# A planner's pace, and stages that are held behind their loads, in a four-layer network whose recurrent scans run beside everything else

## The chip, the cores and the metric

The kernel runs on one core of a Trainium2 chip. The metric is the device time of one launch in microseconds (us), as the median of several runs. A profile is one further execution, recorded by the hardware profiler.

The core's engines each take their instructions strictly in the order of their own queue: TensorE (PE, matmuls; its weight loads are shown as PEld), VectorE (DVE), ScalarE (ACT), GpSimd (POOL) and SyncE (SP). Nearly every DMA of this kernel is issued by SP, so SP's queue orders the transfers, and a wait in it holds back every load behind it.

## The reference, cut to what matters

Four layers work on four images of 1024 positions and 256 channels each. Layers 0 and 3 hold a recurrent scan; layer 1 is a grouped convolution, layer 2 is masked attention and a mixture of eight experts, layer 3 ends with another mixture.

```python
# layer 0, after a norm, a projection to 512 channels, a 3x3 convolution and gelu (x below; N = 64)
dt = softplus(dt_raw @ w_dt + dt_bias);  A = -exp(A_log)
def step(h, inp):                     # 1024 steps for each image
    xt, dtt, Bt, Ct = inp
    h = exp(dtt[:, :, None] * A) * h + (dtt * xt)[:, :, None] * Bt[:, None, :]
    return h, einsum('bdn,bn->bd', h, Ct)
y = ys + x * D_skip                   # then norm, @ w_out, + src
# layer 1: 1x1, grouped 3x3 and 1x1 convolutions with relu, + x
# layer 2: 8 heads; scores where mask else -inf; softmax; @ V; @ Wo; norm; then 8 experts, top 2
# layer 3: x_main, x_gate = split(t @ W_in);  the same kind of scan (N = 16) on silu(x_main @ W_conv)
y = y_seq * silu(x_gate)              # then @ W_out, + t, then 8 experts, top 2
```

## The kernel before, in words

**The scans.** `scans` (L339) runs eight scans one after the other, in the order of `SCANS` (L31): layer 0's for images 0 to 3 and layer 3's for images 0 to 3, here called (0,0), (0,1), (3,0), (0,2), (3,1), (0,3), (3,2), (3,3). A scan is cut into units of 128 rows (channel and state) by 1024 positions: 256 units for layer 0, 64 for layer 3, 1280 in all. For one unit

- SP loads the decay exponents, `dA` (two loads of 256 KB for layer 0, eight of 64 KB for layer 3; five buffers, issued four units ahead),
- ACT takes their exponential two units ahead,
- PE spreads the input over the states into `ps_rep`, one unit ahead (two PSUM buffers),
- DVE multiplies `ps_rep` by B and then scans: the two half steps of a unit, with a `yield` after each,
- POOL multiplies the result `h` by C, and PE collects two units at a time into `ps_y`; ACT copies that out to `yo`.

**The stages.** Everything else is written as generators that yield after a small piece of work, a tick. `STAGES` (L33) lists them: `front` 1 to 3 (layer 0 up to the scan), `middle` 0 to 3 (layer 0's end in `back0`, then `layer1`, `attention`, `moe`, and layer 3 up to its scan in `front3`), `last` 0 to 2 (layer 3's end in `back3`, then `moe`). A stage starts when the scan named beside it is done. The scan and the stages are recorded in one order by hand (a manual schedule): what stands earlier on an engine runs earlier.

**The planner.** `run` (L503) goes through the scan's half steps. It keeps a clock for each of PE, DVE, ACT and POOL: `Metered` (L88) adds an estimated cost for every instruction that is recorded, `matmul_us` (L67) for matmuls. After each half step a clock that is more than `LAG` behind DVE's is pulled up to that distance, and then at most `TICKS` ticks are taken, as long as no clock is ahead of DVE's:

```python
now = clock["vector"]
for e in clock:
    clock[e] = max(clock[e], now - LAG)
for _ in range(TICKS):
    if max(clock.values()) > clock["vector"] + LEAD or self.advance() is None:
        break
```

The value that a tick yields is not used to pace it. When the next scan's inputs are not ready, `need` (L478) takes ticks without pause until they are; the order then has a stretch in which no scan work stands. What is left after the last scan is taken in one go, and `last` for image 3 follows alone, outside the manual schedule.

**The places that the change touches.** `front` (L636) loads x and two weights, sets two pads to zero and goes on to a norm. `back0` (L743) has SP issue 14 loads: the image `tb` (1 MB), the scan's sums `y_back` (eight loads, 2 MB), `u_back` (four, 2 MB) and `w_out` (0.5 MB); two empty ticks follow, then POOL adds rows to `tb`, and DVE adds u times a factor to `y_back`, four instructions. `back3` (L1615) does the same with `gate_back` in the place of u, and POOL multiplies `y_back` by it. `scanned` (L736) issues the `y_back` loads. `attention` (L1048) projects q, k and v, lets POOL add rows to two tiles, and calls `shift` (L1119). That takes the squared norms of q and k on ACT and PE, reduces them on DVE to one number, `large`, which PE, DVE, ACT and SP read into registers (L1159) and branch on (L1161); the other arm is not taken with this data. Only then does SP issue the load of `maskT` (L1101, 2 MB), and `heads` (L1231) runs: for each pair of heads and each of eight key blocks one tick of scores (PE matmuls `ps_sc`, the mask added by a matmul, ACT's exponential `p`) and one of values (`ps_at`). After every two pairs DVE takes a reciprocal of `sums`. `steps` (L540) prepares a scan's inputs: ACT for the softplus (`sp_r`, `sp_e`, `sp_l`), DVE and POOL for its parts, ACT and DVE again for a split into three bf16 parts (`sp_x`, `parts`).

In the profile nearly all of these instructions stand at L120, the line of `Metered` that records them, so groups are told apart by their tiles.

Of the kernel before, what the change touches and what calls it, by code (L numbers as in the profile page):

```python
# [8 lines left out]
BF16 = mybir.dt.bfloat16  # L9
# [7 lines left out]
P = 128  # L17
NB = 4
L = 1024
TB = L // P  # L20
C = 256
DI = 512
DC = DI // P
# [16 lines left out]

LEAD, LAG, TICKS = 0.0, 4.0, 2

# [13 lines left out]
def columns(x):  # L60
    n = 1
    for k in x.shape[1:]:
        n *= k
    return n


def matmul_us(out, lhsT=None, rhs=None, **_):  # L67
    if lhsT is None:
        lhsT = out
    us = 0.46e-3 * columns(out)  # L70
    if lhsT.dtype != BF16:
        us = max(4 * us, 0.3)
    if out.shape[0] <= 32:
        return us / 4
    return us / 2 if lhsT.shape[0] <= 32 else us


def by_columns(per, fixed, of=0):
# [9 lines left out]
class Metered:  # L88
# [21 lines left out]
    def __getattr__(self, key):  # L110
        got = getattr(self.what, key)
        if self.name is None:
            return Metered(got, self.clock, key) if key in self.COST else got
        cost = self.COST[self.name].get(key)
        if cost is None:
            return got

        def run(*args, **kw):
            self.clock[self.name] += cost(*args, **kw)
            return got(*args, **kw)  # L120

        return run


class Hybrid:
# [352 lines left out]
    def need(self, scan):  # L478

        late = False  # L480
        while ("parts", *scan, DC - 1) not in self.ready:
            if self.advance() is None:
                raise RuntimeError(f"{scan} waits for a stage that waits for it")
            late = True
        if late:

            self.clock.update(dict.fromkeys(self.clock, max(self.clock.values())))

    def advance(self):

        if self.stage is None:
            can = [x for x in self.todo if x[2] is None or x[2] in self.done]
            if not can:
                return None
            self.todo.remove(can[0])
            self.stage = getattr(self, can[0][0])(can[0][1])
        cost = next(self.stage, None)
        if cost is None:
            self.stage = None
            return 0.0  # L500
        return cost

    def run(self):  # L503

        self.done, self.ready = set(), set()
        self.todo, self.stage = list(STAGES), None
        nc, tc = self.nc, self.tc
        with tc.tile_pool(name="fps", bufs=1, space=PSUM) as pp:
            self.side_psum(pp)
            for _ in self.front(0):  # L510
                pass
            self.mask_prepare()
        with tc.tile_pool(name="scan", bufs=1) as mp, tc.tile_pool(
            name="scps", bufs=1, space=PSUM
        ) as psum, tc.tile_pool(name="sdps", bufs=1, space=PSUM) as side, tc.manual_schedule():
            self.side_psum(side)
            scatter = self.scatter()
            clock = self.clock = dict.fromkeys(Metered.COST, 0.0)
            self.nc = Metered(nc, clock)
            for n, _ in enumerate(self.scans(mp, psum)):  # L520
                if n % 2:
                    next(scatter, None)
                now = clock["vector"]
                for e in clock:
                    clock[e] = max(clock[e], now - LAG)
                for _ in range(TICKS):
                    if max(clock.values()) > clock["vector"] + LEAD or self.advance() is None:
                        break
            while self.advance() is not None:
                pass  # L530
            self.nc = nc
        assert not self.todo
        with tc.tile_pool(name="lps", bufs=2, space=PSUM) as pp:
            self.side_psum(pp)
            for _ in self.last(NB - 1):
                pass
# [99 lines left out]
    def front(self, b):  # L636
        nc, tc, vec = self.nc, self.tc, self.vec
        R, N = 16, 64
        key = (0, b)
        with tc.tile_pool(name=f"f{b}", bufs=1, side="right") as op:  # L640
# [4 lines left out]
            with tc.tile_pool(name=f"fa{b}", bufs=1, side="right") as fp:  # L645
# [3 lines left out]
                pads = [fp.tile([P, 34, 34], F32, name=f"pad{i}") for i in range(2)]  # L649
                for i in range(2):  # L650
                    nc.gpsimd.memset(pads[i], 0.0)
                yield 1.0
                xT = fp.tile([P, 2, L], F32, name="xT0")
                yield from self.norm(fp, x, TB, x, "ln1")
                yield from self.turned(x, TB, xT, (vec["L0_conv_ln1_g"], vec["L0_conv_ln1_b"]))
# [77 lines left out]
    def image(self, flat, b):  # L733
        return flat[b * L : (b + 1) * L, :].rearrange("(j p) c -> p j c", p=P)

    def scanned(self, pool, key):  # L736
        y = pool.tile([P, DC, L], F32, name="y_back")
        for d in range(DC):
            for c in range(2):
                self.nc.sync.dma_start(y[64 * c : 64 * c + 64, d, :], self.mem["y", *key, d, c])  # L740
        return y

    def back0(self, b, tb):  # L743


        nc, tc, vec = self.nc, self.tc, self.vec
        with tc.tile_pool(name=f"k{b}", bufs=1, side="right") as sp:
            nc.sync.dma_start(tb, self.image(self.a["x"].rearrange("b h w c -> (b h w) c"), b))
            y = self.scanned(sp, (0, b))
            u = sp.tile([P, DC, L], F32, name="u_back")  # L750
            for d in range(DC):
                nc.sync.dma_start(u[:, d, :], self.mem["u", 0, b, d])
            w_out = sp.tile([P, DC, C], F32, name="w_out0")
            nc.sync.dma_start(w_out, self.mem[("w_out0",)])
            yield 2.0
            yield 2.0
            yield from self.add_rows(tb, self.bout0, TB)
            for d in range(DC):
                nc.vector.scalar_tensor_tensor(
                    y[:, d, :], u[:, d, :], vec["L0_conv_D_skip"][:, d : d + 1], y[:, d, :],  # L760
                    ALU.mult, ALU.add,
                )
                yield 1.3
            mv = sp.tile([P, TB, 2], F32, name="b0mv")
            got = {}

            def turn(j):
                got[j] = ps = self.ps("ps_yt")
                for d in range(DC):
                    nc.tensor.transpose(  # L770
                        ps[:, d * P : (d + 1) * P], y[:, d, j * P : (j + 1) * P], self.ident
                    )

            def stats(j):
                st = sp.tile([P, 6], F32, tag="b0st", name="b0st", bufs=2)
                nc.vector.bn_stats(st, got.pop(j))
                nc.vector.bn_aggr(mv[:, j, :], st)

            yield from self.pipe(range(TB), turn, stats, cost=1.0)
            r = self.rstd(sp, mv[:, :, 1], 1e-5, TB, "b0")  # L780
            yield 0.8

            def project(j):
                got[j] = ps = self.ps("ps_o")
                for d in range(DC):
                    nc.tensor.matmul(
                        ps[:, :C], lhsT=y[:, d, j * P : (j + 1) * P], rhs=w_out[:, d, :],
                        start=(d == 0), stop=(d == DC - 1),
                    )

            def add(j):
                nc.vector.scalar_tensor_tensor(
                    tb[:, j, :], got.pop(j)[:, :C], r[:, j : j + 1], tb[:, j, :], ALU.mult, ALU.add
                )

            yield from self.pipe(range(TB), project, add, cost=1.7)
# [251 lines left out]
    def attention(self, b, tb):  # L1048
        nc, tc, vec = self.nc, self.tc, self.vec
        with tc.tile_pool(name=f"at{b}", bufs=1, side="right") as op:  # L1050
# [3 lines left out]
            v = op.tile([P, TB, C], F32, name="v")  # L1054
            mT = op.tile([P, 2, L], BF16, name="mT")
            wo = self.weight(op, "L2_attn_Wo", 2)
            with tc.tile_pool(name=f"aa{b}", bufs=1, side="right") as fp:
                wq, wk, wv = (self.weight(fp, "L2_attn_" + n, 2) for n in ("Wq", "Wk", "Wv"))
                xT = fp.tile([P, 2, L], F32, name="xTa")
# [32 lines left out]
                    nc.scalar.copy(v[:, 2 * j : 2 * j + 2, :], ps)  # L1092

                yield from self.pipe(range(TB // 2), values, cost=1.7)
            yield from self.add_rows(xa, self.bo, TB)
            yield from self.add_rows(tb, self.beta, TB)
            with tc.tile_pool(name=f"ab{b}", bufs=1, side="right") as fp:
                yield from self.shift(fp, qT, kT, mT)
            with tc.tile_pool(name=f"ac{b}", bufs=1, side="right") as fp:
                maskT = fp.tile([P, TB, L], BF16, name="maskT")  # L1100
                nc.sync.dma_start(maskT, self.mem[("maskT",)].rearrange("j p f -> p j f"))  # L1101
                yield 1.0
                for nh in range(2):
                    raw, sums = (
                        fp.tile([P, 2, 512], F32, tag=t, name=t) for t in ("raw", "sums")
# [13 lines left out]
    def shift(self, fp, qT, kT, mT):  # L1119
# [30 lines left out]
        nc.vector.tensor_scalar(most[:, 0:1], most[:, 0:1], -1.0, 1.0, ALU.mult, ALU.add)  # L1150
        large = fp.tile([1, 1], I32, name="large")
        nc.vector.tensor_copy(large, most[:, 0:1])
        yield 1.0
        yield 1.0
        E = mybir.EngineType
        go = {
            E.PE: nc.tensor, E.DVE: nc.vector, E.Activation: nc.scalar, E.SP: nc.sync,
# [457 lines left out]
    def back3(self, b, tb):  # L1615
        nc, tc = self.nc, self.tc
        with tc.tile_pool(name=f"h{b}", bufs=1, side="right") as sp:
            nc.sync.dma_start(tb, self.mem["t", b])
            y = self.scanned(sp, (3, b))
            gate = sp.tile([P, DC, L], F32, name="gate_back")  # L1620
            for d in range(DC):
                nc.sync.dma_start(gate[:, d, :], self.mem["gate", b, d])
            w_out = self.weight(sp, "L3_attn_W_out", DC)
            yield 2.0
            yield 2.0
            for d in range(DC):
                for g in range(2):
                    cols = slice(g * 512, (g + 1) * 512)
# [101 lines left out]
```

## Time and profile before

| what | us |
|---|---|
| median of 3 runs (7048.52 to 7061.61) | 7055.18 |
| profiled execution, whole | 7061.6 |
| its span, first to last instruction | 7059.5 |
| busy: PE, DVE, ACT, POOL | 5383.6, 5212.0, 3462.1, 3650.0 |
| DVE: 1280 scans of 2.285 | 2924.7 |
| DVE: 1280 multiplies of 1.213 | 1553.0 |
| first scan starts; last POOL product of a scan ends | 317.7; 6646.1 |

The span has five parts: a start without scans (to 318 us), a long stretch in which units follow each other (to 5743), a stall in which scan (3,3) waits for its inputs (to about 6250), the rest of the scans (to about 6643), and a tail in which PE ends the experts of images 2 and 3. A line of a timeline has the start and length in us, the engine, the source line, the operation, its output and inputs with their shapes, and in brackets the idle time of the engine before it with what ended that. A line of a table of waits has the engine and tile that waited, what it waited for, and then the us in total, the times and the longest. "issue" is idle time that ended with nothing the profile can name.

### The profile page before, as it was taken

Reading aid. Unit: us, or ns where it says so; the run is one execution under the profiler, and the core shown is the slowest. Engines: PE = TensorE matmul, PEld = TensorE weight load, DVE = VectorE, ACT = ScalarE, POOL = GpSimd, SP = SyncE. Lnnn points to the kernel's source line nnn. Section 1 sums busy time; section 2 is a strip of 40 time slices with the busy share of each in tenths; the row PEclk is TensorE's granted clock in tenths of the full one; section 3 lists DMA queues with packets and bytes.
Section 4 is the critical chain, followed back from the end, with each engine's and each line's share of the span. In section 5 each row is a group of like instructions: output and inputs, shape, how many; then the busy total and the mean of one; then the engine's idle time right before and its main releaser. Section 6 shows DMA issues by size and latency. Waiting matters only on the chain. (4 is left out here: it accounts for less than half of the span.)

```text
span 7059.5 us, 66331 instructions
## 1 busy us (share of the span) xinstructions
PE 5383.6 (76%) x20516; PEld 2218.2 (31%) x20516; DVE 5212.0 (74%) x4477; ACT 3462.1 (49%) x4162; POOL 3650.0 (52%) x1801
## 2 busy tenths in 40 slices
PE   7185876578898567879779668898698677957979
PEld 3020221032253022224235332242254322513556
DVE  2787898887898986789889877898899831247511
ACT  3254666244477324447658434577386332244511
POOL 1288677664556754555766554556656520045300
PEclk9585876578888567979879778898698889877989
DMA  2355666654456565446656654456666620135421
GB/s 82 77 139 158 161 178 167 169 143 120 115 143 176 160 172 136 119 116 171 176 151 164 178 144 120 115 143 178 165 168 165 162 70 6 44 107 152 113 63 33
DMA packets 395053, 939.03 MB, mean 133 GB/s; under 512 B 83268, under 2 KB 165776, under 8 KB 393040
## 3 DMA queue, kind: packets, MB, share of 16 engines
q1 hardware_dynamic: 392512, 932.10, 49.0%
q8 instruction: 172, 2.82, 0.2%
q0 software_dynamic: 2128, 2.13, 0.2%
q14 instruction: 241, 1.97, 0.1%
HBM read 844.17 MB, written 93.95 MB: 133 GB/s over the span
## 5 line engine op out<-in xcount | busy, mean ns | idle before, releaser
L120 POOL TENSOR_TENSOR h<-h,rows 128x1024 f32<-128x1024 f32 x1280 | 3024.2, 2365 | 2138.8 <-DVE h L120 1756.0
L120 DVE TENSOR_TENSOR_SCAN h<-dA,ps_rep 128x1024 f32<-128x1024 f32 x1280 | 2924.7, 2285 | 228.0 <-issue 94.6
L120 DVE TENSOR_TENSOR ps_rep<-ps_rep,rows 128x1024 f32<-128x1024 f32 x1280 | 1553.0, 1213 | 338.7 <-PE ps_rep L120 317.0
L120 ACT ACTIVATE dA<-dA,A_L_conv_A_log 128x1024 f32<-128x1024 f32 x1024 | 1152.8, 1145 | 695.2 <-DMA dA<-dt 600.6
L120 PE MATMUL ps_rep<-S,spread_L_conv_A_log 96*128 96x512 bf16 x2048 | 763.2, 463 | 899.6 <-DVE h L120 731.7
L120 PE MATMUL ps_y<-h,collect_L_conv_A_log 128*32 128x512 f32 x4096 | 750.2, 755 | 91.1 <-POOL h L120 91.1
L120 ACT ACT_TABLE_LOAD x494 | 633.8, 1283 | 174.7 <-DMA dA<-dt 115.0
L120 PEld LDWEIGHTS <-spread_L_conv_A_log 96*128 96x128 bf16 x2048 | 164.5, 103 | 1661.3 <-DVE h L120 1213.5
L120 PE MATMUL ps_h<-xTm,we 128*128 128x512 f32 x1280 | 605.2, 609 | 7.6 <-ACT h_m L120 6.6
L120 PE MATMUL ps_e<-we,h_m 128*128 128x256 f32 x2560 | 587.9, 381 | 10.1 <-ACT h_m L120 10.1
L120 ACT ACTIVATE p<-ps_sc 128x512 f32<-128x512 f32 x512 | 277.9, 595 | 587.2 <-PE ps_sc L120 573.8
L120 ACT ACTIVATE dA<-dA,A_L_attn_A_log 128x1024 f32<-128x1024 f32 x256 | 293.6, 1148 | 490.1 <-DMA dA<-dt 456.4
L120 PEld LDWEIGHTS ps_e<-we,h_m 128*128 128x128 f32 x2560 | 481.8, 190 | 140.6 <-issue 46.0
L120 PE MATMUL ps_at<-p,v 128*32 128x512 f32 x1024 | 363.6, 627 | 63.1 <-ACT p L120 55.7
L120 PE MATMUL ps_rep<-S,spread_L_attn_A_log 96*128 96x512 bf16 x512 | 191.4, 464 | 280.8 <-DVE h L120 239.2
L120 ACT ACTIVATE h_m<-ps_h,cols 128x512 f32<-128x512 f32 x320 | 216.5, 687 | 302.2 <-PE ps_h L120 299.3
L120 DVE SCALAR_TENSOR_TENSOR tb<-ps_e,cw,tb 128x256 f32<-128x256 f32 x448 | 192.6, 473 | 200.5 <-PE ps_e L120 200.5
L120 PEld LDWEIGHTS ps_h<-xTm,we 128*128 128x128 f32 x1280 | 242.4, 193 | 288.1 <-issue 236.3
L120 PE MATMUL ps_sc<-qT,kT 32*128 32x512 f32 x1024 | 300.7, 663 | 0.0
L120 PE MATMUL ps_at<-p,ones 128*32 128x512 f32 x1024 | 280.1, 627 | 0.0
L120 DVE RECIPROCAL sums<-sums 128x512 f32<-128x512 f32 x16 | 53.6, 3353 | 253.4 <-ACT sums L120 253.4
L120 PEld LDWEIGHTS ps_y<-h,collect_L_conv_A_log 128*32 128x32 f32 x4096 | 98.8, 119 | 450.4 <-issue 234.3
(406 smaller groups left out, 5703.5 us busy)
## 6 DMA issues: line engine op xcount, KB each, us to landing
dA<-dt SPq DMA_DIRECT2D x2048, 256.0 KB
dA<-dt SPq DMA_DIRECT2D x2048, 64.0 KB
we<-in_L_ffn_W_dram SPq DMA_DIRECT2D x64, 512.0 KB
parts<-parts SPq DMA_DIRECT2D x64, 384.0 KB
S<-parts SPq DMA_DIRECT2D x96, 256.0 KB
dt<-sp_r SPq DMA_DIRECT2D x64, 256.0 KB
y<-yo SPq DMA_DIRECT2D x128, 128.0 KB
y_back<-y SPq DMA_DIRECT2D x64, 256.0 KB
```

The costliest lines, as they stand in the source:

```text
L120: return got(*args, **kw)
```

## The change

Five edits:

1. The planner's costs and pace. A matmul's cost gets a fixed part; those with few rows get other factors. `LAG` goes from 4 to 8, and `HEAVY` is new: after a tick that moved any clock by more than 1.5 us, no second tick follows in the same half step.
2. `Hold`: a tick can yield `Hold(n)`, and for n half steps no tick is taken, unless the planner is forced to (in `need`, and after the last scan).
3. `Hold` stands in the place of empty ticks: 8 half steps after the loads of `front`, 4 after those of `back0` and 4 more after its row additions, 5 before the branch in `shift`, 8 after the loads of `back3`.
4. In `back0` and `back3` the loads of `y_back` and of u or gate go out in turns: two of `y_back` and one of the other for each quarter. Their number and size stay.
5. `maskT` moves into a pool that lives through the whole of `attention`, and its load is issued after the projections, before the row additions and `shift`.

```diff
-LEAD, LAG, TICKS = 0.0, 4.0, 2
+LEAD, LAG, TICKS, HEAVY = 0.0, 8.0, 2, 1.5
...
-    us = 0.46e-3 * columns(out)
+    us = 0.07 + 0.42e-3 * columns(out)
     if lhsT.dtype != BF16:
-        us = max(4 * us, 0.3)
+        us = max(4 * us - 0.23, 0.3)
     if out.shape[0] <= 32:
-        return us / 4
-    return us / 2 if lhsT.shape[0] <= 32 else us
+        return 0.28 * us
+    return 0.6 * us if lhsT.shape[0] <= 32 else us
...
+class Hold(int):
+    pass
...
-    def advance(self):
+    def advance(self, forced=False):
+        if self.half < self.until and not forced:
+            return None
...
+        if isinstance(cost, Hold):
+            self.until = self.half + cost
         return cost
...
+                self.half = n
                 for _ in range(TICKS):
+                    before = dict(clock)
                     if max(clock.values()) > clock["vector"] + LEAD or self.advance() is None:
                         break
-            while self.advance() is not None:
+                    if max(clock[e] - before[e] for e in clock) > HEAVY:
+                        break
+            while self.advance(forced=True) is not None:
...
-                yield 1.0
+                yield Hold(8)
                 xT = fp.tile([P, 2, L], F32, name="xT0")
...
-    def scanned(self, pool, key):
+    def scanned(self, pool, key, other, of):
         y = pool.tile([P, DC, L], F32, name="y_back")
         for d in range(DC):
             for c in range(2):
                 self.nc.sync.dma_start(y[64 * c : 64 * c + 64, d, :], self.mem["y", *key, d, c])
+            self.nc.sync.dma_start(other[:, d, :], of(d))
         return y
...
-            y = self.scanned(sp, (0, b))
             u = sp.tile([P, DC, L], F32, name="u_back")
-            for d in range(DC):
-                nc.sync.dma_start(u[:, d, :], self.mem["u", 0, b, d])
+            y = self.scanned(sp, (0, b), u, lambda d: self.mem["u", 0, b, d])
...
-            yield 2.0
-            yield 2.0
+            yield Hold(4)
             yield from self.add_rows(tb, self.bout0, TB)
+            yield Hold(4)
...
             wo = self.weight(op, "L2_attn_Wo", 2)
+            maskT = op.tile([P, TB, L], BF16, name="maskT")
...
                 yield from self.pipe(range(TB // 2), values, cost=1.7)
+            nc.sync.dma_start(maskT, self.mem[("maskT",)].rearrange("j p f -> p j f"))
             yield from self.add_rows(xa, self.bo, TB)
...
             with tc.tile_pool(name=f"ac{b}", bufs=1, side="right") as fp:
-                maskT = fp.tile([P, TB, L], BF16, name="maskT")
-                nc.sync.dma_start(maskT, self.mem[("maskT",)].rearrange("j p f -> p j f"))
-                yield 1.0
...
         nc.vector.tensor_copy(large, most[:, 0:1])
-        yield 1.0
-        yield 1.0
+        yield Hold(5)
...
-            y = self.scanned(sp, (3, b))
             gate = sp.tile([P, DC, L], F32, name="gate_back")
-            for d in range(DC):
-                nc.sync.dma_start(gate[:, d, :], self.mem["gate", b, d])
+            y = self.scanned(sp, (3, b), gate, lambda d: self.mem["gate", b, d])
             w_out = self.weight(sp, "L3_attn_W_out", DC)
-            yield 2.0
-            yield 2.0
+            yield Hold(8)
```

More of the change, by code (lines that the diff above doesn't have):

```diff
@@ L481, in need @@
         while ("parts", *scan, DC - 1) not in self.ready:
-            if self.advance() is None:
+            if self.advance(forced=True) is None:
                 raise RuntimeError(f"{scan} waits for a stage that waits for it")
@@ L505, in run @@
         self.done, self.ready = set(), set()
+        self.half = self.until = 0
         self.todo, self.stage = list(STAGES), None
```

## The prediction

> **What bounds the kernel now.** I read four views: the busy table over stretches cut where the scan's first multiply stops and starts, VectorE's (DVE's) waits in the scan stretch, single timelines around the places that the change touches, and the waits of one place where no consumer blocks. The table's columns are stretch, length, then busy time of PE, weight loads, DVE, ACT and POOL, granted clock, DMA share, GB/s.
>
> ```profile
> 317.70:5743.00 5425.30, 4191.12 (x16349) 1610.91 (x16350) 4626.53 (x3571) 2927.38 (x3412) 3326.22 (x1606) 0.80 0.57 152
> 5743.00:6250.00 507.00, 428.75 (x1597) 183.26 (x1596) 75.26 (x179) 159.50 (x267) 39.52 (x31) 0.92 0.08 26
> 6250.00:6643.00 393.00, 261.80 (x965) 116.90 (x963) 294.32 (x238) 204.04 (x216) 213.99 (x107) 0.76 0.57 151
> 6643.00:7059.50 416.50, 372.04 (x1321) 251.63 (x1320) 59.01 (x150) 76.22 (x114) 17.05 (x13) 0.93 0.15 48
> ```
>
> In the first row DVE works 4626.5 of 5425.3 us: a unit of the scan is a 1.21 us multiply and a 2.28 us scan, so 3.5 us at best. The 799 us of DVE idle there are all that the change can win in this stretch. The second row is the stall before scan (3,3), where PE runs stage middle 3 alone; the last is the tail. The planner lays both versions out when the program is built; from that layout I take only which half step a tick falls in, never a time. It forces 306 ticks in the stall before and 307 after, and leaves 48 and 47 for after the last scan: these two rows stay. DVE's instructions stay the same too, so only the idle counts:
>
> ```profile
> DVE ps_rep L120 <- PE ps_rep L120: 283.8, 191, 15.7
> DVE sp_x L120 <- ACT parts L120: 58.7, 23, 14.2
> DVE y_back L120 <- DMA u_back<-u: 55.0, 4, 14.5
> DVE sums L120 <- ACT sums L120: 41.2, 12, 7.9
> ...
> DVE y_at L120 <- PE ps_wo L120: 17.8, 10, 2.2
> DVE ps_rep L120 <- DMA dA<-dt: 16.1, 3, 5.9
> ...
> DVE tb L120 <- PE ps_o L120: 14.5, 6, 5.4
> ...
> DVE ps_rep L120 <- issue: 5.4, 2, 5.2
> DVE ln_st L120 <- DMA x<-in_x_dram: 4.9, 2, 3.2
> ```
>
> The 283.8 us are PE's queue being late with the scan's input: a mask that has not landed, norms in `shift`, attention.
>
> **Holds at back0 and back3: little or nothing.** Each of the four back0 starts shows 12.6 to 14.5 us of DVE waiting for u (55.0 together). A hold takes this wait away. But SP issues 14 loads there (1 + 2 + 2 + 0.5 MB) ahead of the next dA rows, and the scan needs those. Middle 1, ACT and then DVE:
>
> ```profile
> 2537.35 1.15 ACT L120 ACTIVATE dA<-dA,A_L_attn_A_log 128x1024 f32<-128x1024 f32 x1 [1.50 <-DMA dA<-dt]
> 2563.25 1.15 ACT L120 ACTIVATE dA<-dA,A_L_attn_A_log 128x1024 f32<-128x1024 f32 x1 [24.76 <-DMA dA<-dt]
> ```
>
> ```profile
> 2553.29 2.52 DVE L120 SCALAR_TENSOR_TENSOR y_back<-u_back,cols,y_back 128x1024 f32<-128x1024 f32 x2 [13.81 <-DMA u_back<-u]
> ...
> 2564.34 2.27 DVE L120 TENSOR_TENSOR_SCAN h<-dA,ps_rep 128x1024 f32<-128x1024 f32 x1
> ```
>
> The next dA is ready at 2564.4, and DVE scans it at once. Without the u wait DVE would scan what it has (2539.5 + 2.29 + 1.21 = 2543.0) and wait 21 us for dA; today it waits 13.8 and uses the rest for four u sums (7.1 us). So the hold loses about 7 us here; taking the sums and u in turns moves no byte forward for dA. Stage last 2 shows it pure, since nothing on DVE needs its loads:
>
> ```profile
> DVE h L120 <- DMA dA<-dt: 24.2, 3, 21.8
> ```
>
> Middle 0 runs beside a scan with two loads a unit and ACT two units ahead: DVE would wait from 1405.6 to 1421.3, 15.7 for 12.6, +3. Sum +3 + 3 x 7 = **+24 us**; bounds -55 (the wait just goes) and +32 (four times 8). Back3 in last 0 and last 1: POOL waits for gate, PE for POOL, DVE 11.3 to 12.1 us for PE, then dA: it landed 2.3 us before ACT took it, so **-4** (0 to -26). [...]
>
> **Mask loaded as attention begins: -34 us.** PE waits for it with the scan's input queued behind:
>
> ```profile
> 2768.39 1.01 PE L120 MATMUL ps_sc<-maskT,identb 128*128 128x512 bf16 x2 [10.44 <-DMA maskT<-maskT]
> ```
>
> DVE loses 11.8, 15.6, 15.5 and 15.7 us (58.6). Now the 2 MB go out 14 half steps (25 us) earlier; the row needs 9.2 us from issue (2759.2). But dA queues behind: beside the scans of layer 3 (middles 1 to 3, eight dA loads a unit, SP without a gap) ACT finishes dA 0.2 to 0.4 us before DVE takes it, so some 8 us stay each; beside (0,1) about 1. 58.6 - 25 = 34; bounds 20 and 58.6.
>
> **Hold(5) before the branch: -4 us.** DVE loses 4.9 to 5.9 us at each of four branches. In the first, `large` is written at 1589.57 and read at once; the next DVE work starts at 1597.1. That is the branch, which stays; what goes is SP's wait of 6.8 us for `large`, with dA queued behind it. Bounds 0 and -20.
>
> ```profile
> L1726 PEldq COMPARE_BRANCH  x12: 163/314/5113, 594.3 to 5687.0; - x12
> ```
>
> On PE one such branch lasts 5.1 us. [...]
>
> **Pace of attention (new matmul costs): -38 us.** In `heads`, without the mask, DVE loses 39 + 45 + 47 us in middles 0 to 2. Steadily one key block runs per unit, and PE starts one every 4.0 us (2783.0, 2787.1, 2791.0, 2795.1), 0.97 of it the scan's own; DVE needs 3.7. The layout now spreads 16 blocks over 17.5 units instead of 15: 3.03 x 16/17.5 + 0.97 = 3.74, so the 0.3 us a unit nearly go: 14 to 2 us a middle; `sums` saves 3, since its values tick stands a half step earlier; bursts after pauses grow by 3. 12 x 3, and 2 for the part of middle 3: 38. The extra units are idle ones now, and cost DVE nothing. Bounds 0 and -110.
>
> **One heavy tick a half step: -18 us.** `ps_o`, `y_at` and `ps_e` (14.5, 17.8 and 15.9 us) are DVE waits for a matmul group issued in the same half step. One more half step (1.8 us) between them saves up to 1.8 in each of some 15 large ones, 27; I take 18. Bounds 0 and -48.
>
> **LAG 8: +37 us.** An idle engine may now owe 8 us instead of 4, though time that PE or ACT sat idle does not come back. In `steps` the ticks stand at half steps 0 2 4 6 8 10 15 instead of 0 2 4 6 11 17: ten more close ticks in six passes. A close one costs DVE 2.5 to 2.7 us (`sp_x` in middle 1): +25. Other starts (16 row additions in 4 half steps instead of 10, projections 13 instead of 16): +12. Bounds 0 and +45 for the first; the second is the slower rival's.
>
> **Small ones.** Hold at front: -5 (`ln_st`; the floor is 0). Tail: the eight POOL products (9.8 us) can start with the first gate: -4 (0 to -7).
>
> Sum: -34 - 4 - 4 - 38 - 18 - 5 - 4 = -107, +24 + 37 = +61, **-46 us**. The profiled execution took 7061.6, 6.4 above the median 7055.2 of the runs: 7061.6 - 46 = **7015 us**.
>
> **Rivals.** *The holds do free the scan.* For it: 78 us of DVE wait at back0 and back3 go. Against: last 2's 24.2. If dA comes in time, back0 and back3 are worth -55 and -23 instead of +24 and -4: 98 lower, **6917**. Or `heads` wins all of its bound (-110 for -38): **6943**.
> *Nothing to measure:* attention's waits are only moved, since PE is busy 943 of 1127 us in the scans that it stands beside. Without the -38: **7053**.
> *Slower, by the credit.* LAG 8 lets PE or ACT work bunch after each pause; the input of the scan has two buffers, so DVE stalls beyond 3.5 us of lateness. Some 36 starts after a pause (8 in each of 3.3 middles, and the fronts and lasts), each with up to 4 us more: 144, of which 37 are counted: 7015 + 107 = **7122**. It decides from 2.6 us a start (94 in all, 57 more than counted: 7072). For it: 14.2 us lost to ACT at one tick of front 1. Against: one heavy tick a half step, the two-tick cap.
>
> **How the numbers follow.** A measurement tells about 0.2% (14 us) from no change. Forecast (6970 to 7041) 0.45; holds or attention win more (below) 0.22; nothing (7041 to 7069) 0.15; slower 0.18. Faster 0.67, same 0.15, slower 0.18. The range 6930 to 7085 leaves some 0.1 out on each side; the forecast's own range is 6970 to 7041.
>
> **What would show it.** Right: no wait for u_back, but dA waits of 15 to 22 us on DVE at each back0; no PE wait for maskT; 5 us still lost at each branch; `ps_rep` from PE down by 90 to 130 us; `sp_x` from ACT up by some 20; the stall near 507 and the tail near 416 us. Wrong: if DVE's dA waits stay near 24 us in the scan stretch (the holds win), if `ps_rep` grows (the credit decides), or if the stall moves.

## The result, and the profile after

The changed kernel takes 7097.2 us (median of four runs), the kernel before beside it 7058.4: ratio 1.006, 95% interval 1.0034 to 1.0087. It is **0.6% slower**, where 7015 us was forecast. The profiled execution took 7118.0 us with a span of 7116.2, 21 above the median, so sums over its rows come out some 20 us above the runs.

First the busy table over the four stretches, cut as before (PE, weight loads, DVE, ACT, POOL, granted clock, DMA share, GB/s).

```profile
315.60:5805.00 5489.40, 4191.09 (x16280) 1595.69 (x16356) 4644.77 (x3571) 2838.52 (x3344) 3332.22 (x1606) 0.80 0.58 150
5805.00:6312.00 507.00, 426.50 (x1582) 183.39 (x1594) 75.29 (x179) 161.60 (x270) 41.45 (x33) 0.92 0.08 27
6312.00:6699.00 387.00, 255.26 (x957) 116.33 (x956) 295.32 (x238) 191.32 (x205) 212.79 (x105) 0.75 0.60 153
6699.00:7116.20 417.20, 374.30 (x1324) 253.14 (x1322) 58.56 (x150) 76.61 (x115) 17.07 (x13) 0.93 0.16 48
```

Stall and tail stay (507.0 for 507.0 us, 417.2 for 416.5). The scan stretch is 64 us longer. DVE runs the same 3571 instructions there, but is busy 18.2 us longer, and idle 46 us longer (844.6 for 798.8). DVE's waits there (total us, times, longest):

```profile
DVE ps_rep L120 <- PE ps_rep L120: 244.2, 139, 7.9
...
DVE sp_x L120 <- ACT parts L120: 84.1, 31, 6.8
DVE h L120 <- DMA dA<-dt: 79.0, 120, 17.7
DVE top L120 <- PE ps_n L120: 67.9, 4, 18.2
DVE h L120 <- ACT dA L120: 54.7, 54, 16.7
DVE y_at L120 <- PE ps_wo L120: 24.1, 12, 5.6
...
DVE tb L120 <- PE ps_e L120: 22.3, 25, 3.9
...
DVE ps_rep L120 <- DMA dA<-dt: 14.5, 3, 4.9
...
DVE sums L120 <- ACT sums L120: 12.0, 12, 2.1
```

Gone are the u waits (55.0) and most of sums (41.2 to 12.0); ps_rep lost 40. In their place came dA by DMA (24.4 to 79.0), dA by ACT (16.1 to 54.7), top (14.5 to 67.9: DVE waits for PE, which waits for ACT's squares in shift) and sp_x (58.7 to 84.1). Three of the four branches still cost 14.5 us (the row of ps_rep behind dA by DMA; each of them stands where the branch does). At back0 of middle 1, ACT and then DVE:

```profile
2569.59 1.15 ACT L120 ACTIVATE dA<-dA,A_L_attn_A_log 128x1024 f32<-128x1024 f32 x1 [1.53 <-DMA y<-yo]
2597.48 1.15 ACT L120 ACTIVATE dA<-dA,A_L_attn_A_log 128x1024 f32<-128x1024 f32 x1 [26.74 <-DMA dA<-dt]
```

```profile
2581.30 1.21 DVE L120 TENSOR_TENSOR ps_rep<-ps_rep,rows 128x1024 f32<-128x1024 f32 x1
2598.72 2.29 DVE L120 TENSOR_TENSOR_SCAN h<-dA,ps_rep 128x1024 f32<-128x1024 f32 x1 [16.21 <-DMA dA<-dt]
```

DVE multiplies, then stands 16.2 us for dA, which lies behind the bulk loads (SP issues those from 2568.7 to 2582.3, the next dA loads from 2584.2): the new wait that the forecast named.

### The profile page after: what moved, and what is told of

It is laid out like the page before. It is cut to its first block, busy times and chain, and to the rows that moved or that the text cites. A ratio compares the mean times of both kernels' runs of the same rounds, so it can differ in the third digit from the quotient of the medians.

```text
span 7116.2 us, 66199 instructions
## 1 busy us (share of the span) xinstructions
PE 5374.9 (76%) x20426; PEld 2203.0 (31%) x20516; DVE 5230.8 (74%) x4477; ACT 3363.1 (47%) x4086; POOL 3656.7 (51%) x1801
## 5 line engine op out<-in xcount | busy, mean ns | idle before, releaser
L120 DVE TENSOR_TENSOR ps_rep<-ps_rep,rows 128x1024 f32<-128x1024 f32 x1280 | 1553.7, 1214 | 283.8 <-PE ps_rep L120 263.1
L120 PE MATMUL ps_h<-xTm,we 128*128 128x512 f32 x1280 | 620.9, 616 | 19.2 <-ACT h_m L120 19.2
```

## The experiments

Beside each time stands the ratio to runs of the kernel before on the same chip. Three numbers are worked out from each run's trace: **stall**, from the end of the last scan instruction ahead of the gap to the first behind it (534.1 us before, 532.4 changed); **tail**, from the last scan to the end (416.0 and 417.1); **scans**, the rest from the first scan to the last (5791.7 and 5851.1). **Forced** counts the ticks that `need` takes in the stall; like every half step named below it comes from the layout, as in the forecast. Numbers "in the profiles" compare single executions; the changed kernel's is 21 us above its median, so differences against it below that size are weak.

| run | us | ratio (95%) | scans | stall | tail | forced |
|---|---|---|---|---|---|---|
| changed | 7097.2 | 1.0060 (1.0034-1.0087) | 5851.1 | 532.4 | 417.1 | 307 |
| e1_lag4 | 7126.5 | 1.0099 (1.0082-1.0115) | 5713.3 | 670.5 | 429.7 | 404 |
| e4_old_planner | 7148.9 | 1.0142 (1.0126-1.0157) | 5840.3 | 560.6 | 424.7 | 317 |
| e5_planner_alone | 7060.6 | 1.0012 (1.0003-1.0021) | 5821.7 | 523.0 | 404.7 | 300 |
| e6_mask_alone | 7036.9 | 0.9978 (0.9969-0.9987) | 5772.7 | 535.4 | 416.3 | 306 |
| e7_paced | 7100.6 | 1.0063 (1.0050-1.0076) | 5827.9 | 541.2 | 420.2 | 309 |
| e8_no_back_holds | 7053.5 | 0.9999 (0.9989-1.0008) | 5805.8 | 520.8 | 404.5 | 300 |
| e9_hold5 | 7084.9 | 1.0044 (1.0031-1.0057) | 5787.5 | 558.5 | 423.7 | 319 |
| e3_old_costs | 7207.6 | 1.0223 (1.0209-1.0236) | 5969.5 | 530.1 | 405.4 | 300 |
| e10_thin_pool | 7026.6 | 0.9961 (0.9948-0.9974) | 5747.3 | 535.3 | 417.8 | 307 |
| e2_no_cap | 7120.3 | 1.0096 (1.0082-1.0111) | 5863.1 | 529.5 | 411.3 | 305 |
| e12_turns_mask | 7044.1 | 0.9986 (0.9978-0.9995) | 5782.3 | 535.6 | 416.4 | 306 |
| e11_turns_paced_mask | 7031.5 | 0.9971 (0.9958-0.9984) | 5763.3 | 535.6 | 417.1 | 306 |
| e13_lag8_alone | 7223.8 | 1.0246 (1.0230-1.0261) | 6000.9 | 506.6 | 398.8 | 287 |
| e14_costs_alone | 7024.4 | 0.9964 (0.9950-0.9977) | 5681.9 | 607.0 | 421.5 | 352 |
| e15_cap_alone | 7054.7 | 1.0003 (0.9994-1.0012) | 5786.2 | 541.7 | 417.0 | 308 |
| e16_new_plan_paced_mask | 7054.0 | 1.0007 (0.9996-1.0018) | 5807.7 | 520.6 | 406.8 | 300 |
| e17_costs_mask | 7003.5 | 0.9937 (0.9923-0.9951) | 5663.0 | 602.3 | 422.2 | 351 |
| e18_lag55 | 7078.3 | 1.0037 (1.0023-1.0050) | 5796.8 | 539.4 | 416.0 | 307 |

My first theory was that the planner's credit (LAG 8) makes the loss, its rival that the transfers do.

**e1_lag4: the credit undone.** `LAG = 8.0` becomes `4.0` in the changed kernel.

> The changed kernel with LAG 4 again; holds, turns, early mask, new matmul costs and the one heavy tick stay. Two theories. Credit: the changed kernel loses its time by the bursts that LAG 8 allows; what it took over my forecast is 7097 - 7015 = 82 us, so LAG 4 brings it to about 7015, a ratio of 0.994 to the kernel before, with the sp_x waits on ACT back from 84 to about 59 us and the heads' ps_rep waits smaller. Transfers: the time is lost where the scan's dA rows queue behind bulk loads (dA, on DVE and through ACT, 40 to 134 us) and where the mask's load delays the shift (top 14.5 to 67.9 us); then LAG 4 gives back only the 25 us of sp_x, about 7072 or more, ratio 1.002 to 1.006, and the dA and top waits stay.

Slower still: in the changed kernel LAG 8 wins 29 us. With LAG 4 the scans are 138 us shorter, as credit had it, but the stages are laid out so slowly that middle 3 begins on half step 2388 instead of 2308: 404 ticks are forced for 307, and the stall takes the 138 back. Both theories missed: what is not laid beside the scans returns in the stall.

**e4_old_planner.** In the changed kernel `LAG` is 4, the two lines with `HEAVY` are gone, `matmul_us` is the old one.

> The changed kernel with the whole planner of the kernel before (LAG 4, no limit of one heavy tick, old matmul costs): the holds, the loads in turns and the early mask alone. Credit: the transfers are worth what I forecast for them, -34 (mask) - 4 (branch) + 24 - 4 (back0, back3) - 5 - 4 = -27 us, so about 7031, ratio 0.996. Transfers: they lose what the changed kernel loses, so 7080 to 7100, ratio 1.003 to 1.006, with top near 68 us and dA waits near 130 us on DVE in the scan stretch.

7149, beyond either theory. The dA waits stand as expected, but top is at 22.3 us and not near 68, ps_rep has not fallen, and stall and tail are 26 and 9 us longer than before. e9 takes this run apart.

**e5_planner_alone.** The opposite: the three planner edits on the kernel before.

> The kernel before with the changed planner alone (LAG 8, one heavy tick a half step, new matmul costs); no hold, no turns, the mask at its old place. Credit: this holds the loss, and the transfers' -27 us are missing, so about 7058 + 39 + 27 = 7124, ratio 1.009. Transfers: the planner is worth what I forecast, -38 - 18 + 37 = -19 us, or nothing: 7040 to 7060, ratio 0.997 to 1.000.

+6 us, at the transfers theory's edge. Stall and tail win 22 us (300 forced ticks), the scans lose 30.

**e6_mask_alone.**

```
+            maskT = op.tile([P, TB, L], BF16, name="maskT")
...
+            nc.sync.dma_start(maskT, self.mem[("maskT",)].rearrange("j p f -> p j f"))
             yield from self.add_rows(xa, self.bo, TB)
...
-                yield 1.0
```

> The kernel before with the mask's load alone moved to where attention begins (its tile in the outer pool, the empty tick after it gone). My forecast's step: -34 us, 7024, ratio 0.995; PE's mask waits (58.6 us of DVE idle) gone, about 8 us of dA waits at each of three middles come. Transfers: what the mask's wait gave comes back as waits for dA in ACT, behind which the shift's squares queue, so that top rises by some 50 us: nothing won, 7050 to 7060, ratio 0.999 to 1.000.

-18 us, between the two. Summed over the half steps in which the layout puts each pass, DVE idles 34 us less in heads and its start, but 13 more in the row additions and 12 more in shift; the waits for dA, by DMA and by ACT, rise from 24.4 and 16.1 to:

```profile
DVE h L120 <- DMA dA<-dt: 30.7, 101, 3.9
DVE h L120 <- ACT dA L120: 28.6, 58, 4.9
```

**e7_paced: the loads let out slowly.** In the changed kernel, in place of the holds of 4 and 8 in back0 and back3 and of the one load of the mask:

```
             self.nc.sync.dma_start(other[:, d, :], of(d))
+            yield Hold(2)
...
+                    nc.sync.dma_start(maskT[:, j : j + 1, :], parts[:, j : j + 1, :])
```

> The changed kernel with its bulk loads let out bit by bit instead of at once: at back0 and back3 one pair of y and u or gate each two half steps (a hold of 2 behind each), the mask in eight parts of 0.25 MB, one with each projection of q and k. The bytes, the planner and the length of the stages (422 half steps a middle for 420, 309 forced ticks for 307) stay. Theory queue: the loads cost what they do because the scan's next dA rows stand behind megabytes in one queue; let out slowly, they fit beside the scan. Then the dA waits of 12 to 18 us at back0 and of 13 to 17 at back3, and the top waits of 14 to 18 us go: DMA dA, ACT dA and top together from 202 us to some 90, the time to 7097 - 100 = about 7000, ratio 0.992. Theory bandwidth: the bytes have to pass beside the scan's own either way; the waits are only cut into pieces, 7080 to 7100, ratio 1.003 to 1.006.

The waits did as the queue theory says:

```profile
DVE h L120 <- ACT dA L120: 46.5, 63, 4.6
DVE h L120 <- DMA dA<-dt: 42.6, 111, 4.4
DVE top L120 <- PE ps_n L120: 24.4, 4, 6.1
```

113.5 us for 201.6, and none over 6.1. Yet the time stayed. In the profiles the scans are 23 us shorter, stall and tail 12 longer, and DVE is busy 23 us longer with the same work. So loads issued at once are the cause of these waits, and taking the waits away did not shorten this kernel. That is not a clean test of their worth: some two thirds of the ticks of middles 0 to 2 stand three half steps later here, on the other half of a unit (see e9). The busy time needed an explanation (e10).

**e8_no_back_holds.** Both `Hold(4)` of back0 and the `Hold(8)` of back3 become the empty ticks of before.

> The changed kernel with the holds at back0 and back3 replaced by the empty ticks of before; loads in turns, early mask, branch hold and planner stay. My forecast's step: the two holds cost 24 - 4 = 20 us as dA waits instead of u waits; beside that the layout without them is 8 half steps shorter, forces 300 ticks in the stall instead of 307 and leaves 44 for the tail instead of 48, at 1.74 and 8.7 us a tick 12 and up to 30 us. So 7097 - 20 - 12 - 20 = about 7045, ratio 0.998. If the holds do free the scan: 7097 + 55 - 32 = 7120, ratio 1.009.

7053.5: the holds at back0 and back3 cost 44 us, more than the whole loss. Without them, in the profiles, stall and tail are 12 and 13 us shorter, back0's idle 14, shift's 24. From attention's row additions on, the passes of middles 0 to 2 stand exactly 8 half steps earlier than in the changed kernel, so on the same halves of a unit (what that is worth, e9 shows). The stall's row, cut at the scans:

```profile
5753.90:6274.70 520.80, 421.19 (x1545) 181.92 (x1538) 80.69 (x189) 175.88 (x289) 61.02 (x49) 0.91 0.10 32
```

**e9_hold5.** e4 with one number changed: back0's second hold is `Hold(5)`.

> The kernel of the second run (old planner with the holds, turns and early mask; 7149 us) with one number changed: the second hold of back0 is 5 half steps instead of 4. Nothing else differs than on which half of a scan unit the ticks behind it fall: 15, 4, 5 and 4 of the 34 ticks of the four heads on odd halves instead of 17, 5, 17 and 5, and 8 of the 12 of steps instead of 11; the stage is two half steps longer (319 forced ticks for 317). Theory halves: a heavy tick on the wrong half of a unit holds up the scan's input; then heads and steps lose 11 us a middle less, some 35 us, 7115 or below, ratio 1.009. Theory length: only the holds' length counts; then it is 3 to 6 us slower than the second run, 7152 to 7155, ratio 1.014 to 1.015.

64 us faster by one half step, though two half steps longer a stage: the theory of halves, with nearly twice its price. That the loads of back0 get one half step more is not it: back0 idles DVE no less (79 us for 75). From attention's heads on, the passes of the middle stages now stand as in the mask-alone run, 12 half steps later. DVE's waits of e4, then of e9:

```profile
DVE ps_rep L120 <- PE ps_rep L120: 292.5, 183, 10.2
...
DVE sp_x L120 <- ACT parts L120: 70.6, 23, 14.9
```

```profile
DVE ps_rep L120 <- PE ps_rep L120: 227.2, 197, 11.9
...
DVE sp_x L120 <- ACT parts L120: 55.5, 29, 14.1
```

**e3_old_costs.** The old `matmul_us` in the changed kernel.

> The changed kernel with the old matmul costs; LAG 8, the limit of one heavy tick, holds, turns and early mask stay. Heads are laid out in 13.5 units instead of 17.5, a middle in 386 half steps instead of 420, with 300 forced ticks in the stall instead of 307. My forecast's step: the new costs are worth 38 us, so 7097 + 38 = 7135 less 12 for the stall, ratio 1.009. Rival: the new costs bring nothing in attention, since the first kernel of this study has the heads spread over 18.5 units and loses as much there (55 us in middle 1 beside 56 with the mask alone): then 7097 - 12 = 7085, ratio 1.004.

+110: with LAG 8 the new costs are worth three times what I gave them.

**e10_thin_pool: what stretches DVE.** In the changed kernel POOL's product leaves out 960 of its 1024 columns:

```
-                nc.gpsimd.tensor_tensor(h, h, Cm, ALU.mult)
+                nc.gpsimd.tensor_tensor(h[:, :64], h[:, :64], Cm[:, :64], ALU.mult)
+                self.clock["gpsimd"] += 2.3e-3 * 960
```

> The changed kernel with POOL's product behind each scan (h times its row, 2.34 us) cut to 64 of its 1024 columns, so y is wrong; the planner is still charged the full product, and every tick stays in its half step. It tests why DVE's busy time rose by 20 us with the same instructions. Theory port: a small DVE operation that comes while POOL multiplies ends when POOL ends (the eight r_two end 0.06 to 0.08 us behind a POOL product where they take 2.16 us, and take 0.22 where POOL is idle); 42 us of the changed kernel's DVE time in the scan stretch are such waiting, 24 of the kernel before's. Then they are gone: r_two 0.22 and b_v 0.17 us each, DVE's busy time 40 us down, the time 7097 - 42 = 7055 or below, ratio 1.000 or lower. Rival: the long ones have another cause (the operation ahead of them on DVE); then they stay near 2 us, DVE's busy time stays, ratio 1.004 to 1.006.

First what raised the question, in the changed kernel's timeline: DVE's r_two of 64 columns takes 2.16 us and ends 0.08 us behind POOL's product, the like one after it 0.22.

```profile
2025.66 2.34 POOL L120 TENSOR_TENSOR h<-h,rows 128x1024 f32<-128x1024 f32 x1 [3.20 <-DVE r_rest L120]
...
2025.92 2.16 DVE L120 TENSOR_TENSOR r_two<-r_rest,r_two_m 128x64 f32<-128x64 f32 x1
2028.11 0.22 DVE L120 TENSOR_TENSOR r_two<-r_two,orderf 128x64 f32<-128x64 f32 x1
```

Then that operation's durations (ns, least, median, longest), in the changed kernel and in e10:

```profile
L120 DVE TENSOR_TENSOR r_two<-r_rest,r_two_m x7: 224/2159/2161, 2025.9 to 6511.2; 128x64 f32<-128x64 f32 x7
```

```profile
L120 DVE TENSOR_TENSOR r_two<-r_rest,r_two_m x7: 224/224/225, 1982.1 to 6416.7; 128x64 f32<-128x64 f32 x7
```

The stretching is POOL's doing: not one such operation is left. I count as stretched what is over 0.3 us longer than the shortest of its kind and ends with a POOL instruction that began before it: 23.6 us before, 41.8 changed, 39.5 in e5, 42.4 in e8, 58.6 in e7, 27.6 in e9, 0 in e10. The time fell by 71 us; DVE's busy time from the first scan to the last by 87, of which sp_x, which also runs beside POOL, gave 33 in pieces too small for my count. How much of the 71 us is that, and how much POOL's own queue being shorter, is not separated. By what means POOL's product holds DVE up is not shown.

**e2_no_cap.** The two lines with `HEAVY` go from the changed kernel.

> The changed kernel without the limit of one heavy tick a half step; all else stays. My forecast's step: the limit is worth 18 us, and the layout without it is 6 half steps a middle shorter (305 forced ticks for 307, 47 left for 48): 7097 + 18 - 4 - 3 = 7108, ratio 1.008. Rival: the limit costs more half steps than it saves in waits, 7080, ratio 1.003.

+23, where my sum gave +11: beside LAG 8 the limit is worth at least what I forecast.

**e12_turns_mask and e11_turns_paced_mask.** e6 with the loads in turns; then with the mask in eight parts as in e7.

> The kernel before with the early mask and the loads in turns; no hold, old planner, and the layout of the mask-alone run to the half step. My forecast gave the turns nothing. In the run without the holds of back0 and back3 the u waits on DVE fell from 55 to 35 us, and the idle of back0 from 65 to 57. Theory turns: the first sums no longer wait for all y, so 15 to 20 us less than the mask alone (7037): 7018 to 7022, ratio 0.995. Theory none: dA stands behind the same 5.6 MB, and takes the u wait's place: 7035, ratio 0.997 to 0.998.

> As the run before it, with the mask in eight parts of 0.25 MB, one with each projection of q and k. Theory queue: the 2 MB at once delay dA, behind which ACT's squares and so top wait, and dA itself while the rows are added (13 us of DVE idle more in add_rows, 12 in shift, in the mask-alone run than before); let out slowly, those 25 us go: 6995 to 7000, ratio 0.992, or 20 to 25 us under the run before it. Theory bandwidth: the same time as the run before it within 5 us.

The turns give nothing (7044 for 7037): y_back waits less for u (44 for 53 us), dA by DMA 10 us more. Letting the mask out slowly gives 13 of the 25 us expected; the two intervals still touch. e9 beside e12 shows the price of all the holds by itself, since heads and steps stand on the same halves: 41 us, in the profiles 23 in the stall, 7 in the tail, 5 in the scans.

**e13_lag8_alone, e14_costs_alone, e15_cap_alone.** Each of the planner's three edits alone on the kernel before.

> The kernel before with LAG 8 alone; old matmul costs, no limit of one heavy tick, no hold, mask at its old place. Its layout is shorter (372 half steps a middle for 406, 287 forced ticks in the stall for 306, 42 left for the tail for 50): 33 us less in the stall at 1.74 us a tick and about 20 less in the tail. My forecast put LAG 8 at +37 us of DVE waits: 7054 + 37 - 53 = 7038, ratio 0.998. Theory bursts: after each pause the work bunches far more than I counted; the slower rival's full price is 144 us: 7054 + 144 - 53 = 7145, ratio 1.013, with DVE waiting at the starts of every pass (attended, front3's and layer1's projections, moe) and in heads, laid out in 14 units instead of 15.

> The kernel before with the new matmul costs alone (LAG 4, no limit). The layout is longer: heads in 18.5 units each for 15, 440 half steps a middle for 406, 352 forced ticks for 306, 53 left for 50: 80 us more in the stall at 1.74 a tick, 8 in the tail. My forecast's step, -38 us of waits in attention: 7054 - 38 + 88 = 7104, ratio 1.007. Theory none: the heads lose per block and not per unit, and win less than 10 us: 7054 - 8 + 88 = 7134, ratio 1.011. If the longer heads take other work's waits away too: 7080, ratio 1.004.

> The kernel before with the limit of one heavy tick a half step alone (LAG 4, old costs). The layout is 8 half steps a middle longer, 308 forced ticks for 306. My forecast's step: -18 us of waits, +3: 7039, ratio 0.998. Theory halves: the passes behind a tick that is put off begin on the other half of a unit (attended on half step 147 and in 8 half steps, before on 144 and in 7; front3's projections on 322 instead of 315), which costs what it cost between two runs above, 64 us: 7100, ratio 1.007, with DVE waits up at attended, front3's projections and one of the heads (22 of its 34 ticks on odd halves).

LAG 8 alone costs **172 us**: the scans are 209 longer, of which stall and tail give 45 back. The new costs alone win **28**, with a stall 73 longer and scans 110 shorter. The limit alone: nothing, where the halves theory gave it 46 us more; e9's price of a half does not carry over as it stands. The scan stretch and its largest wait, LAG 8 first, then the costs:

```profile
315.90:5943.20 5627.30, 4296.65 (x16488) 1606.61 (x16490) 4639.20 (x3573) 2919.79 (x3417) 3329.78 (x1607) 0.79 0.56 147
```

```profile
DVE ps_rep L120 <- PE ps_rep L120: 352.4, 185, 12.7
```

```profile
312.20:5636.10 5323.90, 4142.62 (x16136) 1568.50 (x16140) 4619.77 (x3565) 2915.69 (x3393) 3319.47 (x1598) 0.81 0.59 155
```

```profile
DVE ps_rep L120 <- PE ps_rep L120: 180.3, 109, 13.6
```

For 283.8 us of ps_rep before, LAG 8 has 352.4 and the costs 180.3. With LAG 8 each of the four heads idles DVE 19 to 33 us in the first three middles; before, the second and fourth idle 7 to 10. Both runs also put other ticks on the other half: of a head's 34 ticks 4 or 5 stand on one half before, 12 to 16 with LAG 8, 11 or 12 with the costs. So 172 and 28 are the price of the constant with the layout that it brings.

**e16_new_plan_paced_mask.** e8 with the mask in eight parts.

> The changed kernel without the holds at back0 and back3 and with the mask in eight parts, one with each projection: the two losses that the runs above have found taken away, the new planner kept. Without the holds it took 7054. Theory queue: top (48 us there) and the ACT dA waits go by some 25 us: 7029, ratio 0.996. Theory bandwidth: 7050 to 7054, ratio 1.000. If POOL's product is as often in the way as in the run with the let-out loads (59 us of stretched DVE operations there, 42 here), 15 us of it are lost again: 7045.

Nothing: top falls from 47.7 to 33.4 us, but ps_rep rises from 198.1 to 212.2. The 13 us of e11 do not carry over.

**e17_costs_mask and e18_lag55.** The kernel before with the new costs and the mask early in eight parts; then with `LAG = 5.5`.

> The two edits that won alone put together: the kernel before with the new matmul costs (7024 us alone) and the mask early, in eight parts (21 us with the turns); LAG 4, no limit, no hold, no turns. The layout is that of the costs alone (351 forced ticks for 352). If the gains add: 7024 - 20 = 7004, ratio 0.993. If the longer heads already take the mask's gain (heads idle there 17 to 31 us in the first head, 10 to 13 in the others, so some 10 us of mask waiting are left in each middle): 7015 to 7024, ratio 0.995 to 0.996.

> As the run before it with LAG 5.5. The layout has 307 forced ticks for 351 and 49 left for 53, so 77 us less in the stall and some 8 in the tail. Theory bursts: credit costs from the first us on, in the scans beside which the ticks stand; LAG 8 for 4 cost the kernel before 209 us in the scans, so 1.5 of 4 costs about 78, and what the stall gives the scans take: 7000, ratio 0.993, equal to the run before it within 15 us. Theory threshold: bursts hurt only beyond the 3.5 us of lateness that the scan's two input buffers cover, and this is still under it: 6930 to 6960, ratio 0.983 to 0.987.

The gains add: 7003.5, ratio **0.9937**, the fastest here, ahead of both kernels. LAG 5.5 puts 44 ticks from the stall beside the scans; the stall gets 63 us shorter and the scans 134 longer. Both theories fell: no threshold at 3.5 us shows, and the first 1.5 us of LAG cost more than my proportion (78). Divided by the 44 ticks, a moved tick saves 1.4 us in the stall and costs 3.0 beside the scans. The halves are hardly the reason in the heads: there the two layouts differ in at most 4 of a head's 34 ticks, e4 and e9 in 12 of the third head's.

## Why the prediction was wrong, point by point

The forecast was -46 us, +39 came: a miss of 85. No single term carries it. Measured apart, the change has three parts: the planner's edits together +6 for a forecast of -19 (e5), the holds at back0 and back3 +44 for +20 (changed less e8), the mask -18 for -34 (e6). They make 32 of the 39 us, and 65 of the 85. The other 20 are the -13 that I gave the branch, front and the tail, and a rest of 7 that lies within the spread of these runs; e12 gives the turns about nothing, and the holds at front and at the branch were not run apart. The three parts were measured in different company, planner and mask on the kernel before and the holds in the changed one, so that they nearly add is not proof that they must.

The step that failed first is **"LAG 8: +37 us"**, with the rule behind it that a constant of the planner has a price of its own, made of DVE waits alone. Alone LAG 8 costs 172 us (in the profiles 209 more in the scans, 45 less in stall and tail); the slower rival named the mechanism, "by the credit", and priced it at 144 at most. In the changed kernel LAG 8 wins 29 (e1). The second is **the holds at +20**, priced as one wait put in the place of another, with the half steps that they empty at nothing.

- **Planner: forecast -38 - 18 + 37 = -19, measured +6.** The three terms do not stand apart: LAG 8 is +172 alone and -29 in the changed kernel, the costs -28 alone and -110 there, the limit 0 alone and -23 there. That the sum came within 25 us is luck. "Other starts +12" was too small: by the half steps in which the layout puts each pass, the changed kernel idles DVE about 15 us more at layer1's and 15 at front3's projections than the kernel before, and some 10 more each at attended and in the fronts. This split depends on the half step to which a wait is put, and is rough. The half on which a pass begins, worth 64 us between e4 and e9, I did not price at all.
- **Holds: forecast +24 - 4, measured +44, for another reason.** dA did take the u wait's place, with waits of 12 to 18 us, where I said 15 to 22; but back0's idle went from 65 to 70 us only, +5 for +24. What I missed is the half steps: while a hold lasts nothing else is taken, so its work comes later, 25 us of it in the stall and the tail. I read that forced ticks stay near 306 and concluded that the holds cost none; they stay because the new planner takes six away (300 in e5) and the holds put seven back. Besides, shift idles DVE 24 us more with the holds (top 67.9 for 47.7 us) and back0 14; why shift does is open.
- **Mask: forecast -34, measured -18.** What came back was sized right, 25 us of DVE idle in the row additions and in shift. The gain was not: heads and their start lost 34 us of idle where I had 58.6, presumably since other waits for PE stand behind the mask's; ps_rep fell by 30 in e6. In the changed kernel top costs 53 us more, 18 of which the planner makes without the mask (32.8 in e5).
- **"DVE's instructions stay the same too, so only the idle counts": wrong by 18 us.** The instructions are the same, their durations are not, since ticks moved onto POOL's products.
- **Branch: right that it stays.** The branches still cost 4.7 to 4.9 us each; the hold's own 4 us were not measured apart. The forecast's row shows the long branch (5.1 us) on PE alone. In the first of the four, in the kernel before, ACT's and SP's branches took 0.06 us, but their next instructions too came only 5 us later (at 1596.6 and 1596.5, ahead of the end of PE's branch at 1596.7). What each engine stands for there is not shown.
- **The sum's base.** 7015 counts from the profiled execution (7061.6); from the median of the runs, which is the metric, it would have been 7009.
- **What was right besides:** no u wait, no mask wait on PE, ps_rep down (by 40 where I said 90 to 130), sp_x up by 25 (20), stall and tail as before. None of the three signs for "wrong" came (dA waits near 24, ps_rep growing, the stall moving), and yet the kernel is slower: they looked at waits and at the stall, and not at what fills DVE's idle time or at DVE's own durations.

Open: which tick's half costs how much, and so how much of each planner constant is its layout. The 64 us between e4 and e9 are shown; their division between PE's queue and POOL's products (11 us of it) is only summed from the profiles.

## What to carry to other kernels

Where fill-in work is laid beside a bottleneck engine, a planner constant has no price of its own: run it alone and in the company it will have (LAG 8: +172 and -29 us), and count what it moves into or out of the serial stretches. In three pairs of runs that differ in LAG a forced tick took 1.4 us of stall, and the same tick laid beside the scans 1.4 (e1 and changed), 3.0 (e17 and e18) or 11 (before and e13), so a shorter stall was never a gain in itself. A hold that empties half steps was paid for later, even where it ended a visible wait (55.0 us of u waits went, and the holds cost 44 us by e8); and loads issued at once only made the next consumer of the same queue late (ACT stood 26.7 us for dA behind 5.5 MB). Before taking an engine's busy time as fixed, look for the same small instruction with two durations (here 0.22 and 2.16 us).

## What the hardware showed unasked

- A 128x64 DVE comparison of two tiles (r_two) took 0.22 us, and 2.16 us when a 2.34 us POOL multiply began 0.26 us ahead of it (changed kernel); with POOL's multiply cut to 64 columns (e10) all seven took 0.22. The scans and the multiplies by B did not show it: in the changed kernel all 1280 scans took 2.23 to 2.29 us and all 1280 multiplies 1.20 to 1.23. What sets the two kinds apart is not shown.
- 5.5 MB issued at once on SP's queue kept a dA row of 0.5 MB away from ACT for 26.7 us (changed kernel, middle 1); let out in groups of 1 MB each two half steps (e7), no wait of DVE's scans for dA exceeded 4.6 us.
